# Places, PSUM banks and buffers of the inverse stage in a four-layer convolution chain (fp32)

## The chip, the cores and the metric

One core of one Trainium2 chip runs the whole kernel in one launch. The metric is device time in microseconds (us); the time before is the median of three runs, 2917.45 us (2915.74 to 2919.48). Engines are named as in the profile: PE is the matrix engine (PEld its weight loads), DVE the vector engine, ACT the scalar engine, POOL GpSimd, SP the engine that issues most of the DMA transfers; ACT issues the rest. "ACTq" and "SPq" are the DMA issues of those two.

## The reference, cut to what matters

The input x has 4 images (batches) of 64 channels of 256 x 256, in fp32. Layers 0, 1 and 3 are long convolutions, layer 2 works in a Haar wavelet basis.

```python
# layers 0, 1, 3: a separable filter per channel, hx and hy from a small network
k = einsum('ijk,imk->ijmk', hx, hy)           # one 256x256 kernel per channel
y = irfft2(rfft2(x, pad) * rfft2(k, pad) / n)[:256, :256]
x = y + x * bias
# layer 2
f1 = haar2d(x)
for i in range(2):
    f4 = einsum('bchw,oc->bohw', f1 * v[i], conv_w[i])   # mixes the 64 channels
    acc += sign(f4) * relu(abs(f4) - tau[i])
x = haar2d(acc, inverse=True) + x
```

As every filter is a product of a filter of rows and one of columns, a convolution is two products with Toeplitz matrices, one along each axis. The inverse Haar transform is a product along each axis too.

## The kernel before, in words

A tile holds one channel, 128 partitions x 512 fp32 (256 kB). Four stages follow for each batch:

- `convolutions`: layers 0 and 1 for each channel (products pa0, py0, pa1, py1), then the pair sums along a row. Sums and differences go to the DRAM tensor `keep`; the differences and the further levels are multiplied by a Haar matrix (`down`, PSUM tile pz), copied on ACT into a tile "co" (`away`, L385) and stored in the DRAM tensor `coef`.
- `mixing`: the channels are mixed for each group of coefficients (PSUM tile px) and shrunk. The result stays in SBUF in z.
- `inverse`: for each channel c, `sooner` loads the Toeplitz tile t2 of layer 3, `early` loads r (what `keep` holds), `fetch` copies the channel out of z on ACT (zc, L525, 1.1 us), `rows` makes four products on PE (pw, L532 and L533). For the first 16 channels of a batch `halves` and `cols` follow (pu, L546). `join` on DVE (L554, L557, L558) adds r and undoes the last pair step; its result is the joined tile u.
- `last`: layer 3 on u. It is five steps: "a3" (product pa on PE), "a3 copy" (ACT, L267, into SBUF), "y3" (product py on PE), "y3 sum" (DVE, L284, adds u times the bias), "out" (the store, L599, issued by ACT). In batches 0 to 2 every third channel (`put_off`, c = 2, 5, 8, ...) is not taken through `last` at once: `aside` stores its u in DRAM, and `convolution` takes it up during the mixing of batch 3. In batch 3 nothing is put off.

The convolutions of batch b+1 run beside the mixing of batch b, and their end, with the copies of coefficients, reaches into the inverse stage of batch b.

**Order.** Each step of each channel is an event with a time in ticks: one tick per channel, plus the step's place in the table PLACE. The events are sorted by time and their instructions written in this order; the framework that builds the kernel then sets, from this order and its own estimate, the final order on every engine. Each engine runs its own instructions strictly in that final order, so a waiting instruction holds all that follows it. In the inverse stage of channel c (turn = start + c, one more for c < 16), `rows` stands at 1.071 ticks, `join` at 1.433, a3 at 2.47, y3 and y3 sum at 3.542, out at 4.537.

**PSUM.** [...] The pool psm (L124) has four tiles of one bank, tag "mm", for pa, py, pz, pw and pu. The pool psx (L125) has two tiles of two banks, tag "mix", for the mixing.

**SBUF.** The tag "y" holds the joined tiles u and the y0 of layer 0, in three buffers. The tag "co" holds both the coefficient copies and the y3 of layer 3, in two buffers. The joined sum t has one ("res").

Of the kernel before, what the change touches and what calls it, by code (L numbers as in the profile page):

```python
# [9 lines left out]
F32 = mybir.dt.float32  # L10
# [7 lines left out]
P = 128  # L18
ROW = S + P

GT = 4
BUFS = {"res": 1, "y": 3, "co": 2}

N_ACT = (14, 12, 12, 6)

PLACE = {
    "load": 0.714,
    "a0": 1.643,
    "a0 copy": 1.643,
    "y0": 2.571,  # L30
    "y0 sum": 2.571,
    "a1": 3.5,
    "a1 copy": 3.5,
    "y1": 4.429,
# [64 lines left out]
def conv_seq_kernel(ctx, tc, x, fz, fw, bias, decay, haar, haar_row, factors, vt, taut, wmix, out):  # L99
# [24 lines left out]
    psm = ctx.enter_context(tc.tile_pool(name="psm", bufs=4, space=PSUM))  # L124
    psx = ctx.enter_context(tc.tile_pool(name="psx", bufs=2, space=PSUM))  # L125
# [115 lines left out]
    def toeplitz(layer, c, name):  # L241

        t = tp.tile([P, 2, S], F32, name=name, tag="toep")
        nc.sync.dma_start(t, ap(pads[layer], c * 2 * ROW, [[1, P], [ROW, 2], [1, S]]))
        return t
# [10 lines left out]
    def first(b, st, key, layer, new):  # L256


        def product(c):
            s = st[c]  # L260
            s["p" + new] = bank(f"p{new}_{b}_{c}")
            contract(s["p" + new], s[key], s[layer][:, 0, :])

        def copy(c):
            s = st[c]
            a = s[new] = io.tile([P, 2, S], F32, name=f"{new}_{b}_{c}", tag="mid")
            nc.scalar.copy(a, s["p" + new])  # L267

        return [product, copy]

    def second(b, st, key, layer, res, new, tag, ahead=None):


        def product(c):
            s = st[c]
            if ahead is not None:
                s[ahead] = toeplitz(ahead, c, f"t{ahead}_{b}_{c}")
            s["p" + new] = bank(f"p{new}_{b}_{c}")
            contract(s["p" + new], s[key], s[layer][:, 1, :])

        def residual(c):
            s = st[c]
            y = io.tile([P, 2, S], F32, name=f"{new}_{b}_{c}", tag=tag, bufs=BUFS[tag])
            nc.vector.scalar_tensor_tensor(y, s[res], bsb[:, layer, c : c + 1], s["p" + new], ALU.mult, ALU.add)  # L284
            s[new] = y

        return [product, residual]
# [6 lines left out]
    def level(n, chunk, begin=0, count=None):  # L294

        count = n if count is None else count
        v = z.rearrange("p n s x c -> p n s (x c)")[:, chunk].rearrange("p (j e s) x -> p j e s x", e=2, s=P // 2 // n)
        halve(v[:, begin : begin + count, 0, 0, :], v[:, begin : begin + count, 1, 0, :])

    def butterfly():  # L300

        v = z.rearrange("p n s (h k) c -> p n s h k c", k=2)
        for h in range(2):
            halve(v[:, :, 0, h, 0, :], v[:, :, 0, h, 1, :])
# [6 lines left out]
    def at(time, run, unit):  # L311
        events.append((time, len(events), run, unit))

    def convolutions(b, ticks, in_parts=(), border=None):
# [67 lines left out]
        def away(c):  # L382
            t = io.tile([P, 2, S], F32, name=f"co_{b}_{c}", tag="co", bufs=BUFS["co"])
            ps = parts.pop(("ps", c)).rearrange("p e (k w) -> p e k w", k=2)
            nc.scalar.copy(t.rearrange("p k (e w) -> p e k w", e=2), ps)  # L385
            nc.sync.dma_start(coef[b][:, c].rearrange("k p w -> p k w"), t)
# [122 lines left out]
    def inverse(b, start, put_off):  # L509

        st = {}

        def early(c):
            r = mx.tile([P, 2, 2, P], F32, name=f"r_{b}_{c}", tag="f", bufs=3)
            nc.sync.dma_start(r, keep[b][c])
            st[c]["r"] = r

        def sooner(c):
            st[c] = {}
            if c not in put_off:  # L520
                st[c][2] = toeplitz(2, c, f"t2_{b}_{c}")

        def fetch(c):
            a = mx.tile([P, 2, 2, P], F32, name=f"zc_{b}_{c}", tag="mag")
            nc.scalar.copy(a.rearrange("p h k i -> p (h k) i"), z[:, c // 16, :, :, c % 16].rearrange("p i x -> p x i"))  # L525
            st[c]["z"] = a

        def rows(c):
            a = st[c]["z"]
            ps = psm.tile([P, 2, 2, P], F32, name=f"pw_{b}_{c}", tag="mm")  # L530
            for m in range(2):
                nc.tensor.matmul(ps[:, 0, m, :], a[:, 0, m, :], hsinv, start=True, stop=True)  # L532
                nc.tensor.transpose(ps[:, 1, m, :], a[:, 1, m, :], ident)  # L533
            st[c]["pw"] = ps

        def halves(c):
            w = st[c]["w"] = mx.tile([P, 2, 2, 2, P], F32R, name=f"w_{b}_{c}", tag="f4")
            ps = st[c]["pw"]
            nc.scalar.copy(w[:, 0], ps)
            nc.vector.tensor_tensor(w[:, 1], ps, w[:, 0].bitcast(F32), ALU.subtract)  # L540

        def cols(c):
            ps = psm.tile([P, 2, 2, P], F32, name=f"pu_{b}_{c}", tag="mm")
            flat = "p e m w -> p (e m w)"
            for i in range(2):
                nc.tensor.matmul(  # L546
                    ps.rearrange(flat), hb, st[c]["w"][:, i].rearrange(flat), start=(i == 0), stop=(i == 1)
                )
            st[c]["pw"] = ps

        def join(c):
            ps = st[c]["pw"]
            t = io.tile([P, 2, 2, P], F32, name=f"t_{b}_{c}", tag="res", bufs=BUFS["res"])
            nc.vector.scalar_tensor_tensor(t, st[c]["r"], 0.5, ps, ALU.mult, ALU.add)  # L554
            u = io.tile([P, 2, S], F32, name=f"u_{b}_{c}", tag="y", bufs=BUFS["y"])
            v = u.rearrange("p m (w e) -> p m w e", e=2)
            nc.vector.tensor_add(v[:, :, :, 0], t[:, 0], t[:, 1])  # L557
            nc.vector.tensor_sub(v[:, :, :, 1], t[:, 0], t[:, 1])  # L558
            st[c]["u"] = u

        def aside(c):
            nc.scalar.dma_start(late[b, c], st.pop(c)["u"])

        along = start - groups - 3

        def when(tick, n, chunk, *span):
            at(tick + PLACE["level"], lambda _: level(n, chunk, *span), 0)

        at(along + 11 + PLACE["level"], lambda _: butterfly(), 0)
        for chunk in range(1, 4):  # L570
            turn = start + 16 * (chunk - 1)
            for n in (1, 2, 4, 8):
                when(along + 12 + 3 * chunk if b + 1 < B else turn, n, chunk)
            when(turn + 1, 16, chunk)
            for i in range(2):
                when(turn + 2 + 2 * i, 32, chunk, 16 * i, 16)
            for i in range(4):
                when(turn + 6 + 2 * i, 64, chunk, 16 * i, 16)

        for c in range(C):  # L580
            for name, stage in zip(("sooner", "early", "fetch", "rows"), (sooner, early, fetch, rows)):
                at(start + c + PLACE[name], stage, c)
            turn = start + c
            if c < 16:
                at(start + c + PLACE["halves"], halves, c)
                at(start + c + PLACE["cols"], cols, c)
                turn += 1
            at(turn + PLACE["join"], join, c)
            if c in put_off:
                at(turn + PLACE["aside"], aside, c)  # L590
            else:
                for name, stage in zip(("a3", "a3 copy", "y3", "y3 sum", "out"), last(b, st)):
                    at(turn + PLACE[name], stage, c)

    def last(b, st):
        return [
            *first(b, st, "u", 2, "a3"),
            *second(b, st, "a3", 2, "u", "y3", "co"),
            lambda c: nc.scalar.dma_start(out[b, c].rearrange("(k p) w -> p k w", p=P), st.pop(c)["y3"]),  # L599
        ]  # L600
# [19 lines left out]
    put_off = range(2, C, 3)  # L620
# [22 lines left out]
    for b in range(B):  # L643
        mixing(b, start, N_ACT[b])
        end = start + groups + 3
        if b + 1 < B:
            ready = convolutions(b + 1, spread(ahead, end + 2), in_parts=range(C), border=end)
        else:
            convolution(
                [(i, c) for i in range(B - 1) for c in sorted(put_off)], spread(start - 2, end + 2, (B - 1) * len(put_off))  # L650
            )
        inverse(b, end, put_off if b + 1 < B else ())

        start = max(end + C, ready + 3)
        ahead = start - 3
# [114 lines left out]
```

## Time and profile before

| | |
|---|---|
| median of three runs | 2917.45 us (2915.74 to 2919.48) |
| the profiled execution | 2913.15 us, of it the profile's span 2911.3 us |
| granted clock of PE in it | 0.997 |
| `fetch` zc (ACT, L525), 256 times | 281.5 us, 1101 ns each |
| a copies (ACT, L267), 768 times | 490.7 us, 639 ns each |
| joined tiles (DVE, L554 from pw), 192 times | 131.6 us, 685 ns each |
| y3 sums (DVE, L284 from u), 193 times | 143.9 us, 745 ns each; idle before them 124.6 us |
| pw products (PE, L532 and L533) | 185.9 and 140.4 us |

A group of the profile is one line and one tile of the program on one engine. In the groups all the products of `contract` have the lines L253 and L254, so they are told apart by the tiles: pa from u and py from a in the inverse stage. A bracket at the end of a timeline row gives the idle time before the instruction and what released it; where an instruction waits for several things, the last one by the profile is named. Matrix products are pipelined, so a row's length is longer than its distance to the next row.

### The profile page before, as it was taken

What the parts mean: (1) busy time and instruction counts of PE and PEld (TensorE: products, weight loads), DVE (VectorE), ACT (ScalarE), POOL (GpSimd) and SP (SyncE); (2) the same over time, 40 slices, a digit from 0 to 9 for tenths busy, and PEclk for the clock granted to TensorE, in tenths of its full rate; (3) what the DMA queues carried; (4) which work ended last, traced back from release to release, by engine and by line L of the source; (5) the groups of instructions that cost most, each with busy time, mean ns of one, the idle gap of its engine ahead of it and who ended that gap; (6) DMA issues with size and microseconds to landing.
All of it is one profiled execution on the core that took longest, in us unless ns stands there. A gap on an engine that the chain in (4) does not pass through costs nothing. (4 is left out here: it accounts for less than half of the span.)

```text
span 2911.3 us, 52368 instructions
## 1 busy us (share of the span) xinstructions
PE 2827.3 (97%) x16566; PEld 2551.1 (88%) x16566; DVE 2499.0 (86%) x4263; ACT 2085.2 (72%) x4950; POOL 329.7 (11%) x644
## 2 busy tenths in 40 slices
PE   8999999999999999999999899999999899999999
PEld 6899998888888898998898898998898898887898
DVE  4656558999998679999998679999998779999985
ACT  2333338999995558989985558998986568887554
POOL 0111111121120001221211001121211000000000
PEclk9999999999999999999999999999999999999999
DMA  5878777666676886777677886777777888776676
GB/s 162 256 229 233 231 233 222 205 205 206 197 213 205 268 260 198 214 213 212 208 214 237 253 269 195 214 215 212 208 212 233 262 278 233 235 233 199 208 237 208
DMA packets 599367, 649.77 MB, mean 223 GB/s; under 512 B 48465, under 2 KB 517044, under 8 KB 598964
## 3 DMA queue, kind: packets, MB, share of 16 engines
q1 hardware_dynamic: 519860, 562.09, 65.2%
q10 hardware_dynamic: 79232, 84.34, 8.2%
q8 instruction: 134, 2.20, 0.3%
q14 instruction: 141, 1.16, 0.1%
HBM read 426.77 MB, written 219.48 MB: 222 GB/s over the span
## 5 line engine op out<-in xcount | busy, mean ns | idle before, releaser
L253 PE MATMUL py<-t,a 128*128 128x256 f32 x3072 | 920.9, 382 | 7.5 <-ACT a L267 6.9
L267 ACT COPY a<-pa 128x512 f32<-128x512 f32 x768 | 490.7, 639 | 430.3 <-PE pa L254 390.5
L465 ACT ACTIVATE f<-px,vt 128x64 f32<-128x64 f32 x2816 | 620.2, 408 | 95.9 <-DVE f L460 95.6
L254 PEld LDWEIGHTS py<-t,a 128*128 128x128 f32 x3072 | 584.3, 190 | 79.8
L254 PE MATMUL py<-t,a 128*128 128x128 f32 x3072 | 590.8, 274 | 0.0
L253 PEld LDWEIGHTS py<-t,a 128*128 128x128 f32 x3072 | 496.2, 191 | 47.5 <-ACT a L267 16.8
L441 PE MATMUL px<-wb,f 128*128 128x256 f32 x2048 | 490.4, 381 | 11.1 <-ACT f L465 10.6
L441 PEld LDWEIGHTS px<-wb,f 128*128 128x128 f32 x2048 | 367.7, 190 | 56.4 <-ACT f L465 17.6
L525 ACT COPY zc<-z 128x512 f32<-128x512 f32 x256 | 281.5, 1101 | 170.6 <-PE pw L533 143.6
L343 POOL TENSOR_TENSOR sd<-less 128x128 f32<-128x128 f32 (+4 forms) x320 | 189.3, 592 | 1884.7 <-DVE less L342 1616.8
L469 ACT ACTIVATE mag<-f 128x1024 f32<-128x1024 f32 x256 | 304.1, 1188 | 21.0 <-DVE z L486 20.4
L476 DVE TENSOR_TENSOR mag<-mag,vt 128x1024 f32<-128x1024 f32 x256 | 312.4, 1220 | 4.6 <-ACT mag L469 3.4
L480 DVE SCALAR_TENSOR_TENSOR mag<-mag,f 128x1024 f32<-128x1024 f32 x256 | 312.7, 1222 | 1.1 <-DVE mag L476 0.5
L253 PE MATMUL pa<-t,y 128*128 128x256 f32 x1024 | 308.5, 383 | 4.7 <-DVE y L284 2.9
L253 PE MATMUL pa<-t,x 128*128 128x256 f32 x1024 | 305.7, 380 | 0.0
L366 DVE TENSOR_TENSOR sp<-sd,sp 128x512 fp32r<-128x512 f32 x256 | 179.1, 700 | 135.0 <-ACT sp L361 133.8
L472 ACT ACTIVATE f<-f 128x1024 f32<-128x1024 f32 x256 | 291.4, 1138 | 3.2
L253 PE MATMUL pa<-t,u 128*128 128x256 f32 x772 | 236.0, 388 | 39.2 <-issue 18.9
L284 DVE SCALAR_TENSOR_TENSOR y<-u,bsb,py 128x512 f32<-128x512 f32 x193 | 143.9, 745 | 124.6 <-PE py L254 101.3
L284 DVE SCALAR_TENSOR_TENSOR y<-x,bsb,py 128x512 f32<-128x512 f32 x256 | 189.8, 742 | 42.7 <-PE py L254 41.7
L254 PEld LDWEIGHTS pa<-t,y 128*128 128x128 f32 x1024 | 194.7, 190 | 26.5
L254 PEld LDWEIGHTS pa<-t,x 128*128 128x128 f32 x1024 | 194.6, 190 | 26.3
(72 smaller groups left out, 4450.8 us busy)
## 6 DMA issues: line engine op xcount, KB each, us to landing
t<-pad SPq DMA_DIRECT2D x768, 256.0 KB, 4.0
x<-in_x SPq DMA_DIRECT2D x256, 256.0 KB, 3.8
coef<-co SPq DMA_DIRECT2D x256, 256.0 KB, 3.0
f<-coef SPq DMA_DIRECT2D x256, 256.0 KB, 3.1
r<-keep SPq DMA_DIRECT2D x256, 256.0 KB, 3.7
out_y<-y ACTq DMA_DIRECT2D x256, 256.0 KB, 4.0
keep<-sums SPq DMA_DIRECT2D x256, 128.0 KB, 2.8
keep<-sd SPq DMA_DIRECT2D x256, 128.0 KB, 2.8
```

The lines of the kernel that those rows point to most:

```text
L253: nc.tensor.matmul(ps[:, m, :], src[:, 0, m * P : (m + 1) * P], t[:, ::-1], start=True, stop=False)
L254: nc.tensor.matmul(ps[:, m, P:], src[:, 1, m * P : (m + 1) * P], t[:, : P - 1 : -1], start=False, stop=True)
L267: nc.scalar.copy(a, s["p" + new])
L284: nc.vector.scalar_tensor_tensor(y, s[res], bsb[:, layer, c : c + 1], s["p" + new], ALU.mult, ALU.add)
L343: engine.tensor_tensor(t[:, :, :, half:length], v[..., 0], v[..., 1], ALU.subtract)
L441: nc.tensor.matmul(ps[:, q, h, :], f[:, q, h * P : (h + 1) * P], wb.rearrange("p r n -> p (r n)"), start=True, stop=True,)
L465: nc.scalar.mul(f4[:, j], px[:, j], scale(g, 0)[:, j : j + 1])
L469: nc.scalar.activation(mag, st[g]["f4"], AF.Abs)
L472: nc.scalar.activation(st[g]["f4"], st[g]["f4"], AF.Sign)
L476: nc.vector.tensor_sub(mag, mag, over(g, 1, 16))
L480: nc.vector.scalar_tensor_tensor(mag, mag, 0.0, st[g]["f4"], ALU.max, ALU.mult)
L525: nc.scalar.copy(a.rearrange("p h k i -> p (h k) i"), z[:, c // 16, :, :, c % 16].rearrange("p i x -> p x i"))
```

## The change

Three things, all in the inverse stage: the row products pw take a tile of the mix's PSUM pool and use its first bank; the joined tiles' tag "y" has five buffers in place of three; and the steps of `last` are moved. Where channels are put off, the first of three channels keeps the places of a3 and a3 copy, and has y3, y3 sum and out 0.32 ticks earlier; the second has a3 and a3 copy 0.5 ticks later and y3, y3 sum and out 0.18 ticks later. In batch 3, where nothing is put off, y3, y3 sum and out of every channel come 0.5 ticks earlier.

```diff
-BUFS = {"res": 1, "y": 3, "co": 2}
+BUFS = {"res": 1, "y": 5, "co": 2}
...
         def rows(c):
             a = st[c]["z"]
-            ps = psm.tile([P, 2, 2, P], F32, name=f"pw_{b}_{c}", tag="mm")
+            ps = psx.tile([P, 2, 2, 2, P], F32, name=f"pw_{b}_{c}", tag="mix")[:, 0]
...
             if c in put_off:
                 at(turn + PLACE["aside"], aside, c)
             else:
+                shift = (0.0, -0.32) if c % 3 == 0 else (0.5, 0.18)
+                if not put_off:
+                    shift = (0.0, -0.5)
                 for name, stage in zip(("a3", "a3 copy", "y3", "y3 sum", "out"), last(b, st)):
-                    at(turn + PLACE[name], stage, c)
+                    at(turn + PLACE[name] + shift[name[0] != "a"], stage, c)
```

## The prediction, made before the changed kernel was run

> **What bounds the kernel now.** I read the page's first part, then a table of windows of 20 us, then the timeline inside the windows where TensorE (PE) has gaps, then the idle column of the instruction groups.
>
> ```profile
> PE 2827.3 (97%) x16566; PEld 2551.1 (88%) x16566; DVE 2499.0 (86%) x4263; ACT 2085.2 (72%) x4950; POOL 329.7 (11%) x644
> ...
> 980.00:1000.00 20.00, 16.97 (x108) 15.11 (x109) 14.00 (x28) 11.81 (x15) 0.00 (x0) 1.00 0.74 234
> ...
> 1040.00:1060.00 20.00, 19.82 (x139) 18.55 (x138) 15.38 (x30) 11.73 (x13) 0.00 (x0) 1.00 0.90 284
> ...
> 2840.00:2860.00 20.00, 20.00 (x137) 18.75 (x136) 12.68 (x24) 10.35 (x13) 0.00 (x0) 1.00 0.78 244
> ```
>
> PE sets the time, and only its gaps can be won: 84 us in all. A window row gives the stretch, then busy PE, PEld, DVE, ACT and POOL, the granted clock, the DMA share and GB/s. The change touches only the inverse stages: batch 0 near 880-1080, batch 1 near 1540-1740, batch 2 near 2200-2400, batch 3 near 2680-2907. From the rows, PE idles 13.6, 10.7 and 10.4 us in the first three and 4.5 us in the last (all of it before 2800). I split the first three: phase A (channels below 16, with the column products) holds 13.1 us, phase B (the coefficient copies of the next batch still run) 21.4 us, phase C (after them) 0.2 us. So the whole prize is about 35 us, and phases C and the last 100 us of the kernel can only lose.
>
> Phase B, from the timeline (start, length, engine, line):
>
> ```profile
> 984.30 0.59 ACT L385 COPY co<-pz 128x512 f32<-128x512 f32 x1 [1.19 <-PE pz L373]
> ...
> 984.91 0.37 SPq L386 DMA_DIRECT2D coef<-co  x1
> ...
> 988.72 0.75 DVE L284 SCALAR_TENSOR_TENSOR y<-u,bsb,py 128x512 f32<-128x512 f32 x1 [1.02 <-DMA coef<-co]
> ...
> 989.49 0.38 ACTq L599 DMA_DIRECT2D out_y<-y  x1
> ...
> 990.24 0.67 PE L253 MATMUL pa<-t,u 128*128 128x256 f32 x2 [1.00 <-PE pw L533]
> ```
>
> The result tile y3 and the coefficient tile share the tag "co" with two buffers. The second y3 of three channels waits for the coefficient store (988.72), DVE stands behind it, the next join is late, and PE waits 1.00 us. The cycle of three channels is 9.30 us (984.30 to the next such copy at 993.60), while PE's own work is 3 rows of 0.66 + 4 products of 1.31 + 0.55 for pz = 7.8 us (start-to-start distances in the timeline).
>
> **The change, part by part.** No instruction is added or removed; only order, banks and buffers move.
>
> *Five joined tiles.* What the third buffer cost is bounded by the row of the join:
>
> ```profile
> L557 DVE TENSOR_TENSOR u<-t 128x256 f32<-128x256 f32 x256 | 108.2, 423 | 6.7 <-DMA late<-u 1.2
> ```
>
> A join that waits for an old u to be stored shows 1.2 us in the whole run: worth 0 to -1.2 us, I take 0. Its effect is indirect: joins may run further ahead.
>
> *Row results in the mix banks.* Before, four banks serve 8 tiles per three channels (3 pw, 2 pa, 2 py, 1 pz); afterwards they serve 5, and pw has two tiles of its own, which the mix leaves unused here. rows(c) then waits for join(c-2), placed 1.64 ticks earlier, so nothing new is on the path; at the borders the first pw waits until the mix's last tile is read and the next mix's first tile waits for the join of channel 62, both done a tick before (0 to +1 us per border, taken as 0). Gain: part of phase A, where PE waits for u behind a DVE that is busy 18.8 to 19.9 of 20 us (860-900). More banks don't shorten DVE. Bounds -9 and +3 us (the latter from the shorter covers below); I take -3.
>
> *Even spacing, batches 0 to 2.* The places become a3 at 2.47 and 3.97, y3 at 3.222 and 4.722 ticks. That spreads the two y3, but it also shortens what PE has between a3 and y3 of one channel. In the built order of PE, before: another product and a row product (1.97 us). After: in phase C a row product and a third (0.88 us) for one channel, one and a half (0.99 us) for the other. What is needed shows where the trace has the two products back to back:
>
> ```profile
> 2669.33 0.39 PE L254 MATMUL pa<-t,v 128*128 128x128 f32 x2
> ...
> 2669.75 0.58 ACT L267 COPY a<-pa 128x512 f32<-128x512 f32 x1 [0.70 <-PE pa L254]
> ...
> 2670.39 0.70 PE L253 MATMUL py<-t,a 128*128 128x256 f32 x2 [0.68 <-ACT a L267]
> ```
>
> pa's stream ends at 2669.55 (it began at 2668.24, plus 1.31); the copy starts 0.20 later (0.25 in the last stage: 2898.79 against 2898.54), lasts 0.58, and py starts 0.06 after it, with its first pair 0.1 longer. So a cover of x us leaves PE idle about 1.0 - x. Phase C: 0.12 us in each of some 9 cycles, three batches: **+3 us** (0 to +6).
>
> Phase B after the change. PE's loop: 7.8 + 0.35 (cover 0.66) + 0.12 (cover 0.88) = 8.25 us, because DVE's waiting y3 now holds the join of a product that stands later on PE. The loop over the one shared buffer stays, as the change adds none: copy to y3 4.42 us (984.30 to 988.72), y3 to its store 0.77, the store's landing 2.7 (median of 975-1010), then the next copy: 7.9 us. But a faster stage loads the DMA: 9 transfers of 262 kB in 8.25 us are 286 GB/s. The row for that is 1040-1060 (284 GB/s, share 0.90), and out_y lands there after 4.9 us: the loop is then 10.1 us, no gain. So between -1.05 and 0 per cycle, about 18 cycles in three batches (4, 7 and 7 gaps of this kind): -19 to 0. I take -0.45 per cycle, **-8 us**, since loop and load must meet between 8.25 and 9.3.
>
> [...] The rows agree that a buffer is short, but it is "co", not "y" or PSUM[...]. [...] The landing times above already stretch from 2.7 to 4.9 us at 284 GB/s, so I follow the rows.
>
> *Even spacing, batch 3.* Nothing is put off there, y3 moves 0.5 tick forward: 0.57 tick behind its own a3. In the built order before, PE runs row(c+1), a3(c), y3(c-1): a3 is covered by 3.28 us. After: a3(c), one row product, y3(c), and for the last six channels (58-63) a3 and y3 with nothing between, as the rows now run six channels ahead. The trace of before in this stage:
>
> ```profile
> 2842.47 0.38 PE L254 MATMUL pa<-t,u 128*128 128x128 f32 x2
> ...
> 2842.69 0.60 PE L253 MATMUL py<-t,a 128*128 128x256 f32 x2
> ...
> 2842.95 0.58 ACT L267 COPY a<-pa 128x512 f32<-128x512 f32 x1 [0.22 <-PE pa L254]
> ```
>
> PE goes straight on with the py of another channel at 2842.69; if it were its own, a would be there at 2843.6. On ACT, the store of an earlier y3 and the next fetch (1.10 us) stand around the copy, but the store's y3 is done a product earlier and the fetch fits behind, so the copy starts at once. SP's queue: a t2 load waits for the py six channels earlier, and r loads stand behind it; in the new order both are still issued four channels (13 us) before use and land in 3.8 us, cost 0. Channels 37-57: 21 x 0.34 = 7.1 us; 36: 0.2; 58-63: 6 x 1.0 = 6.0; together 13 us in a stretch where PE is 20.00 of 20. Channels 0-31 lose 9 us by the same count, but there DVE is full (20.00 of 20 at 2700-2740) and PE has 4.5 us idle and slower matmuls (123 to 130 in 20 us instead of 136), so most is hidden: +3. **+16 us**, bounds +8 (ACT and PE overlap better than in the row) and +24 (nothing hidden).
>
> Sum: -3 + 3 - 8 + 16 = +8 us. The profiled execution took 2913.15 us (span 2911.3, 1.85 us around it) and would become 2921. Its time lies 4.3 us below the median 2917.45; on the median the forecast is 2926.
>
> **The rivals.**
> *Phase B wins all, and batch 3 hides half*: -17 (landings stay at 2.7 us), -6 in A, +2, +8: -13, so **2904**. For it: the loop of 7.9 us as measured, DMA share only 0.74 in the worst window. Against: the landing of 4.9 us. It decides once three channels take under 8.6 us in phase B.
> *The parts cancel*: phase B -8, batch 3 only +8, A and C zero: **2917**. For it: ACT is half idle in batch 3. Against: the latency row, which is ACT-free too.
> *ACT's order costs more*: in phase B the store of the second y3 now stands ahead of the next a3 copy, so a wait for "co" holds ACT and PE instead of a fetch. One landing of 4.9 us delays that copy by up to 1 us past its cover: B +3, batch 3 +22, C +4: +29, **2947**. Against: that copy is not due before 6.15 us into the cycle, the store is issued by 6.
>
> **How the numbers follow.** Main case 0.49 (own range 2919 to 2934), all of B won 0.18, cancel 0.21, ACT's order 0.12. Within 0.2% means 2911.6 to 2923.3, about what a measurement of this kernel can tell from no change. Slower: 0.12 + most of the main case + a tail of cancel, 0.57; same 0.24; faster 0.19. The range 2905 to 2944 cuts half of the two outer cases.
>
> **What would show it.** Batch 3: idle before py, released by ACT's a, of about 0.3 us per channel, near 1 us in the last six, the windows after 2800 at 18 of 20. Phase B: copies of co 8.5 to 9 us apart instead of 9.3, y3 still released by coef or out_y, out_y landing later. Phase C full within 2%. I am wrong if py in batch 3 shows no wait for a, or if phase B falls to 8.3 us.

## The result, and the profile after

The changed kernel takes 2917.12 us (median of 14 runs, 2914.62 to 2921.9) against 2916.57 us before (14 runs): ratio 1.000, 95% interval 0.9992 to 1.0009. No difference can be measured. The profiled execution took 2915.48 us, its span is 2913.7 us (before 2911.3), and the granted clock rose from 0.997 to 1.000.

The unchanged sum hides two large changes that cancel. The marks of the trace cut the span into stages: the first copy of a channel out of z (L525) begins an inverse stage, the first instruction of the next mixing (L452) or the end of the span ends it. The mixing stages are the same within 0.8 us.

| inverse stage, us | batch 0 | batch 1 | batch 2 | batch 3 |
|---|---|---|---|---|
| before | 211.4 | 209.1 | 203.4 | 235.6 |
| after | 203.2 | 205.2 | 202.4 | 251.3 |
| difference | -8.2 | -3.9 | -1.0 | +15.7 |

One stage of one execution is good to about 3 us: batch 2, 203.4 us before, took 206.8 us in the run below that moves steps of batch 3 alone.

First the busy totals of the page and the table of windows, both after (columns as before: busy PE, PEld, DVE, ACT, POOL, then clock, DMA share, GB/s):

```profile
PE 2837.4 (97%) x16566; PEld 2548.3 (87%) x16566; DVE 2504.6 (86%) x4263; ACT 2081.6 (71%) x4950; POOL 329.1 (11%) x644
...
980.00:1000.00 20.00, 18.66 (x122) 16.80 (x121) 14.10 (x28) 12.51 (x16) 0.00 (x0) 1.00 0.86 271
...
1040.00:1060.00 20.00, 20.00 (x138) 18.83 (x137) 15.13 (x30) 12.12 (x15) 0.00 (x0) 1.00 0.92 290
...
2840.00:2860.00 20.00, 19.67 (x123) 17.31 (x122) 11.77 (x22) 8.92 (x11) 0.00 (x0) 1.00 0.78 221
```

The first window gained (122 matrix products in place of 108), the second kept its pace, the last one lost: 123 products in place of 137, though PE still counts as busy for 19.67 us. Read the count, not the busy time: rows of products are longer than the distance between them (the row at 2841.99 below takes 0.39 us, the next begins 0.22 us after it), so a short wait disappears in the overlap. The weight loads (PEld) show a part of it, 17.31 us in place of 18.75. The groups of the page (busy time, mean ns | idle before, releaser) name what is late, first before, then after:

```profile
L253 PE MATMUL py<-t,a 128*128 128x256 f32 x3072 | 920.9, 382 | 7.5 <-ACT a L267 6.9
...
L253 PE MATMUL pa<-t,u 128*128 128x256 f32 x772 | 236.0, 388 | 39.2 <-issue 18.9
```

```profile
L253 PE MATMUL py<-t,a 128*128 128x256 f32 x3072 | 929.8, 384 | 32.1 <-ACT a L267 28.8
...
L253 PE MATMUL pa<-t,u 128*128 128x256 f32 x772 | 231.4, 381 | 1.5 <-PE pw L533 0.7
```

The wait has moved from the first product of a channel (pa) to the second (py), which needs the copy a. The timeline of batch 3 after (start, length, engine, line) shows one channel and the next:

```profile
2841.99 0.39 PE L254 MATMUL pa<-t,u 128*128 128x128 f32 x2
2842.21 0.39 PE L532 MATMUL pw<-hrow,zc 128*128 128x128 f32 x2
2842.47 0.59 ACT L267 COPY a<-pa 128x512 f32<-128x512 f32 x1 [1.87 <-PE pa L254]
...
2843.10 0.30 PEld L253 LDWEIGHTS py<-t,a 128*128 128x128 f32 x2 [0.30 <-ACT a L267]
2843.10 0.70 PE L253 MATMUL py<-t,a 128*128 128x256 f32 x2
...
2846.08 0.59 ACT L267 COPY a<-pa 128x512 f32<-128x512 f32 x1 [1.87 <-PE pa L254]
```

From copy to copy it is 3.61 us. Before, it was 3.28 us, from the copy at 2842.95 that the prediction shows to the next:

```profile
2846.23 0.58 ACT L267 COPY a<-pa 128x512 f32<-128x512 f32 x1 [0.22 <-PE pa L254]
```

After, only the row product (0.66 us) stands between a3 and y3 of one channel, py starts 0.04 us after its copy has ended, and 0.33 us per channel are lost. The product py carries no bracket, so no idle time is put down to it; its weight load waited 0.30 us for ACT's a.

The starts of the y3 sums (DVE) split the last inverse stage by channels:

| batch 3, us | before | places put back (first run below) | after |
|---|---|---|---|
| first copy to y3 of channel 31 | 129.1 | 121.9 | 131.3 |
| channels 31 to 36 | 16.4 | 16.4 | 18.3 |
| channels 36 to 57 | 69.0 | 69.0 | 76.1 |
| channels 57 to 63 | 17.1 | 17.1 | 21.7 |
| from there to the end | 4.1 | 4.1 | 3.9 |

### The profile page after: what moved, and what is told of

Read it like the earlier page. It is cut to its first block, busy times and chain, and to the rows that moved or that the text cites. A ratio compares the mean times of both kernels' runs of the same rounds, so it can differ in the third digit from the quotient of the medians.

```text
span 2913.7 us, 52472 instructions
## 1 busy us (share of the span) xinstructions
PE 2837.4 (97%) x16566; PEld 2548.3 (87%) x16566; DVE 2504.6 (86%) x4263; ACT 2081.6 (71%) x4950; POOL 329.1 (11%) x644
## 5 line engine op out<-in xcount | busy, mean ns | idle before, releaser
L525 ACT COPY zc<-z 128x512 f32<-128x512 f32 x256 | 279.7, 1101 | 49.5 <-PE pw L533 38.0
```

## The experiments

Differences in us are worked out from the ratio, as (ratio - 1) x 2917. Edits are shown against the kernel before, except where the text says against the changed kernel.

**Batch 3's places put back** (against the changed kernel).

```diff
                 if not put_off:
-                    shift = (0.0, -0.5)
+                    shift = (0.0, 0.0)
```

> The changed kernel with the places of batch 3 as they were before (a3 at 2.47, y3 at 3.542); banks, buffers and the spacing of batches 0 to 2 stay. Theory (a3's copy lost its cover in batch 3): the inverse stage of batch 3 falls back from 251.3 to about 235.6 us, py waits for a only a few us, the whole is 14 to 16 us faster than the changed kernel: 2901 to 2903. Rival (the loss in batch 3 comes from the row products' two tiles or from joins that run ahead): the stage stays near 250 us and the time near 2917.

2893.06 us, ratio 0.992 (0.9906 to 0.9935): -23 us against the kernel before, more than the theory's 14 to 16. Its last stage took 228.4 us in place of 251.3, the first three 203.3, 206.6 and 199.9. So batch 3's places cost 22.9 us, and the other parts of the change won as much, 7 us of it in the last stage, where the theory had expected nothing from them.

**Batch 3's places alone.**

```diff
+                shift = (0.0, 0.0)
+                if not put_off:
+                    shift = (0.0, -0.5)
...
-                    at(turn + PLACE[name], stage, c)
+                    at(turn + PLACE[name] + shift[name[0] != "a"], stage, c)
```

> The kernel before with only y3, y3 sum and out of batch 3 half a tick earlier. Theory: in the built order y3 then follows its own a3 on PE with nothing between, for nearly all 64 channels; at 1.0 us each, less some 10 us hidden behind DVE before 2800, the stage grows by 40 to 55 us: about 2960 to 2970. Rival (the places cost nothing by themselves): within 5 us of 2917.

2971.25 us, ratio 1.0183 (1.0168 to 1.0198): +53 us; the last stage took 290.3 us, 54.7 more than before. In the timeline of this run nothing stands between the two products of a channel:

```profile
2862.30 0.38 PE L254 MATMUL pa<-t,u 128*128 128x128 f32 x2
2862.78 0.59 ACT L267 COPY a<-pa 128x512 f32<-128x512 f32 x1 [0.20 <-PE pa L254]
2863.42 0.70 PE L253 MATMUL py<-t,a 128*128 128x256 f32 x2 [0.73 <-ACT a L267]
...
2867.06 0.59 ACT L267 COPY a<-pa 128x512 f32<-128x512 f32 x1 [0.20 <-PE pa L254]
```

A channel takes 4.28 us, 1.00 more than 3.28. Together with the 3.61 us above (cover 0.66, loss 0.33) this is the prediction's rule, idle = 1.0 - cover, at two points. Counted over all 64 channels in the built order it gives 23.0 us for the changed kernel (measured 22.9) and 61 for this one (54.7; the rest is missing among the channels up to 31, which lost 21 us of the 29 counted). Why the same places leave a cover in the one and none in the other: with pw in banks of its own, the builder sets a row product between the two; that was read from the built order, not tried.

**Banks and five tiles, no step moved.**

```diff
-BUFS = {"res": 1, "y": 3, "co": 2}
+BUFS = {"res": 1, "y": 5, "co": 2}
...
-            ps = psm.tile([P, 2, 2, P], F32, name=f"pw_{b}_{c}", tag="mm")
+            ps = psx.tile([P, 2, 2, 2, P], F32, name=f"pw_{b}_{c}", tag="mix")[:, 0]
```

> The kernel before with the row products in the mix's banks and five joined tiles, all places as before. Theory (the gain of batches 0 to 2 comes from the spacing in phase B, and banks help phase A only): 2 to 5 us faster, 2912 to 2915, with copies of co still about 9.3 us apart in phase B. Rival (banks and buffers make the gain): 12 to 15 us faster, near 2903, copies of co 8.3 to 8.6 us apart.

2902.14 us, ratio 0.9945 (0.9932 to 0.9958): -16 us. The theory missed and the rival's value came, but not the rival's mark: in phase B the coefficient copies come 9.84 us apart (mean of three gaps per batch; 9.52 before), so this gain lies outside phase B.

**Even spacing of batches 0 to 2 alone.**

```diff
+                shift = (0.0, -0.32) if c % 3 == 0 else (0.5, 0.18)
+                if not put_off:
+                    shift = (0.0, 0.0)
...
-                    at(turn + PLACE[name], stage, c)
+                    at(turn + PLACE[name] + shift[name[0] != "a"], stage, c)
```

> The kernel before with only the spacing of batches 0 to 2. Theory: phase B wins as in the changed kernel, but with the row products back in the common banks PE has just one row product (0.66 us) between a3 and y3 of every channel, 0.35 us lost each, some 6 us per batch in phase C: -8 + 15, about +5 to +10, 2922 to 2927. Rival (spacing alone makes the gain): 8 to 13 us faster, 2904 to 2909.

2922.02 us, ratio 1.0012 (1.0003 to 1.0020): +3.5 us. Alone the spacing is a small loss. With banks and tiles it wins: 0.992 against 0.9945, some 7 us, though the two intervals just meet. The theory had both halves, with a sum just below its 5 to 10: in phase B the coefficient copies come 8.82 us apart in place of 9.52, and phase C loses. In this run the built order leaves 0.66 us between a3 and y3 of every channel, and where the coefficient copies have ended, PE makes 383, 411 and 320 products in stretches (1005-1066, 1665-1730, 2320-2370 us) that held 410, 440 and 340 before; the changed kernel, with more cover, makes 413, 435 and 340.

**Banks alone, and five tiles alone.** 
```diff
-            ps = psm.tile([P, 2, 2, P], F32, name=f"pw_{b}_{c}", tag="mm")
+            ps = psx.tile([P, 2, 2, 2, P], F32, name=f"pw_{b}_{c}", tag="mix")[:, 0]
```

```diff
-BUFS = {"res": 1, "y": 3, "co": 2}
+BUFS = {"res": 1, "y": 5, "co": 2}
```

> The kernel before with the row products in the mix banks alone: three joined tiles, no place moved. Banks and buffers together gave -14.5 us against the kernel before (2902.1 against about 2916.6), -6.8 of it in the last inverse stage by the stage times and about -5 in the first three. Theory 'the banks make that gain': 2902 to 2905, last inverse stage near 229 us instead of 235.6. Rival 'the five joined tiles make it': 2914 to 2917, last inverse stage near 235. If both are needed together (joins run ahead only when pw has banks of its own and u has tiles): 2908 to 2914 here and 2915 to 2917 with five tiles alone.

> The kernel before with five joined tiles alone. PE's order is the same as before; only the order of some DVE instructions in the convolutions' end and the waits for old joined tiles differ. Theory 'the banks make the gain of banks and buffers': 2915 to 2917, no change, as the prediction's row of 1.2 us says. Rival 'the tiles make it': 2902 to 2905.

Banks: 2902.46 us, ratio 0.9953 (0.9940 to 0.9965), -14 us. Tiles: 2912.33 us, ratio 0.9984 (0.9978 to 0.9991), -5 us, a small gain that the row of 1.2 us did not show. So the banks make most of the gain. Whether the tiles add to it the times can't tell: both together gave -16 us, and the interval, -20 to -12, holds -14 as well as -19. In the last stage the tiles do add: it took 232.8 us with the banks alone (229 was expected), 232.5 with the tiles alone and 228.8 with both; the four other runs with the banks, four or five tiles and batch 3's old places lie between 228 and 230 us, the five with neither between 234.8 and 235.6. What the tiles change there was not followed; they leave the order on PE as it was and change that on DVE at 114 of 4263 places. Part of the banks' gain can be seen at the start of batch 3. The timeline and the window there, before:

```profile
2675.72 2.08 ACT L525 COPY zc<-z 128x512 f32<-128x512 f32 x2 [1.82 <-DVE z L486]
2676.86 0.80 PE L532 MATMUL pw<-hrow,zc 128*128 128x128 f32 x2 [3.58 <-ACT zc L525]
...
2678.30 1.06 PE L253 MATMUL py<-t,a 128*128 128x256 f32 x2
```

```profile
2672.00:2683.00 11.00, 7.42 (x31) 6.63 (x30) 10.81 (x14) 5.23 (x8) 0.00 (x0) 0.69 0.37 110
```

and with the banks alone:

```profile
2669.54 0.60 PE L253 MATMUL py<-t,a 128*128 128x256 f32 x2
...
2671.70 0.49 PE L532 MATMUL pw<-hrow,zc 128*128 128x128 f32 x2 [1.33 <-ACT zc L525]
...
2673.71 0.59 PE L253 MATMUL pa<-t,v 128*128 128x256 f32 x2
```

```profile
2666.00:2678.00 12.00, 9.64 (x60) 8.18 (x59) 11.91 (x19) 8.96 (x12) 0.00 (x0) 1.00 0.59 161
```

Before, the first row product stands ahead of a py whose input is ready (its copy ended at 2673.89), waits 3.58 us for the first copy out of z, and the products behind it are slow: a pair of 128x256 takes 1.06 us in place of 0.60, the granted clock of the window is 0.69. With the banks that py goes first, PE idles 1.33 us, and the clock of the window is 1.00. The first y3 of the stage comes 13.4 us after the first copy, in place of 16.7: 3.3 us. How much of this is the clock can be read from a run further down, the third shared buffer. Its PE runs in the order of before and waits as long at this place, but the clock stays at 1.00:

```profile
2653.15 0.49 PE L532 MATMUL pw<-hrow,zc 128*128 128x128 f32 x2 [3.59 <-ACT zc L525]
```

```profile
2653.15:2658.15 5.00, 4.92 (x32) 4.45 (x33) 5.00 (x6) 3.14 (x4) 0.00 (x0) 1.00 0.18 51
```

There the first y3 comes after 15.6 us, and the stage takes 234.8 us in place of 235.6. So the slow products are an estimated 1.1 us of the 3.3 (16.7 less 15.6), and less than 1 us of the stage; the rest of the 3.3 us goes with the order.

The first three stages together are 4.4 us shorter with the banks alone (619.5 against 623.9), with 31 or 32 products in place of 26 or 27, and of 21, in the two slices of 5 us of batches 1 and 2 in which PE has its first gaps. With 2.8 us in the last stage that is 7.2 us; the traces do not place the other half of the 14 us, as the profiled execution of before lies 3.7 us below its median and that of this run 2.7 us above. Where that half sits stays open.

**A buffer of its own for y3.**

```diff
-BUFS = {"res": 1, "y": 3, "co": 2}
+BUFS = {"res": 1, "y": 3, "co": 2, "yo": 2}
...
-            *second(b, st, "a3", 2, "u", "y3", "co"),
+            *second(b, st, "a3", 2, "u", "y3", "yo"),
```

> The kernel before with a tag of its own (two buffers) for the y3 of layer 3, so that coefficient copies and y3 no longer wait for each other's stores; PE's order is unchanged. Theory 'the shared tag sets phase B' (the prediction's loop of 7.9 to 10.1 us): the coefficient copies of the first inverse stage come 8.0 to 8.6 us apart instead of 9.3, no y3 in that stretch is released by coef, and the first three stages together lose 10 to 18 us: 2899 to 2907. Rival 'the transfers themselves set phase B': copies stay 9.0 to 9.3 apart and y3 waits for its own older store: 2912 to 2917. Rival 'PE's order sets it': no wait of y3 is left, the join is still late, 2912 to 2917.

2888.23 us, ratio 0.990 (0.9887 to 0.9914): -29 us, more than the theory's 10 to 18. The coefficient copies come 8.13 us apart in phase B, as the theory had it. The first three stages took 202.2, 200.1 and 195.6 us (9.2, 9.0 and 7.8 less), the last 235.5, where no coefficient copies are left. The order of PE's instructions is that of before.

**A third shared buffer; and one copy buffer with two for y3.**

```diff
-BUFS = {"res": 1, "y": 3, "co": 2}
+BUFS = {"res": 1, "y": 3, "co": 3}
```

```diff
-BUFS = {"res": 1, "y": 3, "co": 2}
+BUFS = {"res": 1, "y": 3, "co": 1, "yo": 2}
```

> The kernel before with three buffers for the shared tag of coefficient copies and y3. The order on every engine is that of the run with a tag of its own for y3 (2888.2 us); only the waits for old buffers differ. Theory 'the loop over the two shared buffers costs, and one more breaks it': the copies of phase B come 8.1 us apart as there, 2887 to 2892. Rival 'it is the mixing of two kinds in one ring that costs, however many buffers': still 9.0 or more apart, 2905 to 2917.

> The kernel before with two buffers of their own for y3 and only one for the coefficient copies: three in all. Same order on every engine as with two and two (2888.2 us). Theory 'y3's wait for the coefficient store is what counts': 2887 to 2891, since in phase B the copies come one in 8.1 us and each store lands within 3 to 6 us. Rival 'the copies need two buffers': where two copies follow within a channel (before phase B) ACT waits a landing of 3 to 5 us for the first: 2893 to 2905.

Third shared buffer: 2888.45 us, ratio 0.9893 (0.9877 to 0.9910), -31 us. One number in one line wins what the separate tag wins. One copy buffer: 2895.76 us, 0.9916 (0.9902 to 0.9931), -25 us; the inverse stages are as short as with two, but the first mixing starts at 454.0 us of the trace in place of 450.8 and lasts 2 to 3 us longer, so the rival came, near the small end of its range. Phase B with the third shared buffer, first the windows, then the timeline:

```profile
980.00:1000.00 20.00, 19.76 (x132) 18.04 (x131) 15.62 (x31) 13.60 (x17) 0.00 (x0) 1.00 0.91 286
1000.00:1020.00 20.00, 20.00 (x141) 18.88 (x140) 15.05 (x31) 12.49 (x15) 0.00 (x0) 1.00 0.95 303
```

```profile
988.25 0.59 ACT L385 COPY co<-pz 128x512 f32<-128x512 f32 x1 [1.19 <-PE pz L373]
...
990.79 0.74 DVE L284 SCALAR_TENSOR_TENSOR y<-u,bsb,py 128x512 f32<-128x512 f32 x1
...
995.92 0.75 DVE L284 SCALAR_TENSOR_TENSOR y<-u,bsb,py 128x512 f32<-128x512 f32 x1 [1.21 <-PE py L254]
996.38 0.59 ACT L385 COPY co<-pz 128x512 f32<-128x512 f32 x1 [1.19 <-PE pz L373]
```

The copies come 8.13 us apart in all three batches, the second y3 of the three channels (990.79) waits for nothing, and 132 products stand where there were 108. The transfers did not become faster: in 960-1005 us the stores of y3 land after 4.7 us (median) and those of coefficients after 5.1, against 4.4 and 4.4 before. They are just not waited for. (With a buffer of its own for y3 as with the third shared one, the builder also sets some y3 sums ahead of a join, which changes DVE's order at 30 of 4263 places; the orders on PE and ACT are those of before. That order and the missing wait come together and were not parted.)

**All but batch 3's places, with a tag of its own for y3; then the same with no step moved.** Both have the row products in the mix banks, four joined tiles, one copy buffer and two for y3. Against the changed kernel:

```diff
-BUFS = {"res": 1, "y": 5, "co": 2}
+BUFS = {"res": 1, "y": 4, "co": 1, "yo": 2}
...
-                    shift = (0.0, -0.5)
+                    shift = (0.0, 0.0)
...
-            *second(b, st, "a3", 2, "u", "y3", "co"),
+            *second(b, st, "a3", 2, "u", "y3", "yo"),
```

and the second without the lines of `shift`.

> The changed kernel with the last inverse stage's places put back, four joined tiles, one buffer for the coefficient copies and two of their own for y3. With the places put back alone it was 2893.1. Theory 'the shared tag still costs after the change': phase B goes from copies 8.3 to 9.0 apart to about 8.0 to 8.25, some 0.5 us in each of 18 cycles: -5 to -9, 2884 to 2888. Rival 'after the even spacing nothing waits for the shared tag any more': 2892 to 2895. Rival 'one buffer for the coefficient copies is too few' (each copy waits for the landing of the one before, 3 to 5 us, and two copies follow each other within a channel): slower than 2897.

> The best version so far (2876.4 us) without its places: the kernel before with the row products in the mix banks, four joined tiles, one buffer for coefficient copies and two of their own for y3, all steps where they stood before. Theory 'once the shared buffer is gone, the places have nothing left to win': banks alone gave -14.4 and the tag alone -28.6; if they add, 2873 to 2877. Rival 'the even spacing still pays when the waits are gone' (it paid 9 us with the banks: 2893.1 against 2902.1): 2882 to 2888. Rival 'banks and tag win the same idle time': 2884 to 2889, the same number, told apart by phase B: copies 8.1 apart for this one against above 8.4 for the other.

2876.39 us, ratio 0.9861 (0.9848 to 0.9875), and without the places 2877.28 us, ratio 0.9853 (0.9838 to 0.9868). The first is 17 us faster than the run with batch 3's places put back (2893.06 us), so the shared buffer still cost that one some 17 us, more than the 5 to 9 expected, and once it is gone the even spacing is worth nothing. Spacing and buffer seem to win the same idle time; banks and buffer add, within the intervals (-14 for the banks, -25 to -29 for y3's own tag, -43 together with four joined tiles).

**The version that beats both: banks, four joined tiles, third shared buffer, nothing moved.**

```diff
-BUFS = {"res": 1, "y": 3, "co": 2}
+BUFS = {"res": 1, "y": 4, "co": 3}
...
-            ps = psm.tile([P, 2, 2, P], F32, name=f"pw_{b}_{c}", tag="mm")
+            ps = psx.tile([P, 2, 2, 2, P], F32, name=f"pw_{b}_{c}", tag="mix")[:, 0]
```

> The kernel before with the row products in the mix banks, four joined tiles and three buffers for the shared tag of coefficient copies and y3; no step is moved. Same order on every engine as the run with banks and own tags and no places (2877.3 us), whose single copy buffer cost ACT waits before the first mixing (there the first mixing starts at 453.8 us of the trace instead of 450.8, and the first one lasts as long as before). Theory 'the third shared buffer is enough, and the copies are free again': 3 us better, 2872 to 2876, first mixing at 450 to 451. Rival 'with the joins earlier three shared buffers are again too few for copies and y3 together': y3 released by coef in phase B, 2878 to 2888.

2871.54 us (2865.8 to 2873.07), ratio 0.9845 (0.9831 to 0.9858): -45 us. The windows of phase B and the group of pa:

```profile
960.00:980.00 20.00, 20.00 (x133) 18.55 (x132) 15.35 (x31) 14.17 (x18) 0.00 (x0) 1.00 0.94 299
980.00:1000.00 20.00, 20.00 (x136) 18.55 (x135) 15.73 (x31) 12.69 (x15) 0.00 (x0) 1.00 0.93 288
```

```profile
L253 PE MATMUL pa<-t,u 128*128 128x256 f32 x772 | 233.8, 385 | 2.4 <-PE pw L533 1.8 <-issue 0.4
```

PE is full there, idle time before pa is 2.4 us in place of 39.2, and the clock is 1.000.

## Why the prediction was right or wrong, point by point

The time, 2917.1 us, lies in the range; the likeliest case, 2926, did not come. The value is that of "the parts cancel", but not for that case's reason: batch 3 lost 15.7 us, not 8. That the time lies in the range is in part luck. The runs put -16 us on banks and tiles (predicted -3), some -7 on the even spacing (predicted -5) and +23 on batch 3's places (predicted +16): two errors, of 13 and of 7 us, with opposite signs.

- **Batch 3, +16: right in mechanism, and its total right by two errors.** The places cost 22.9 us. Behind channel 31 the table shows 7.1 us for channels 36 to 57, as predicted to the tenth; 1.9 before them and 4.6 behind (predicted 0.2 and 6.0), 13.6 in all against 13. The term "most is hidden: +3" failed: channels up to 31 lost 9.4 us (131.3 against 121.9), all that the cover count gave. That DVE was busy there hid nothing in this kernel; it hid 8 of 29 us where nothing at all stood between the products. Of the signs, idle time before py released by a came, the windows at 18 of 20 did not: the wait hides in the rows. The other error is in the next point: the prediction gave the banks nothing in this stage, and banks and tiles won 7.2 us there (235.6 to 228.4).
- **Banks, -3 with bounds -9 and +3: failed.** Alone they win 14 us (10 to 17). "At the borders 0 to +1 us per border, taken as 0" is one term: at the last border the first y3 comes 3.3 us sooner, because the builder's order there changes and, for an estimated 1.1 us of it, because the slow products are gone (the clock of the window is 1.00 in place of 0.69). The row that told it, 3.58 us in front of pw, was in the trace but in no sum: the wait ends at 2676.86, and the prediction's last stage starts at 2680. Its "4.5 us in the last" are other gaps, 4.0 us of them between 2740 and 2760. Where half of the 14 us sits stays open.
- **Five tiles, 0 to -1.2 us: too small alone** (-5 us). On top of the banks the times can't tell, and the last stage shows some 4 us (232.8 to 228.8). The waits that are put down to an old u, 1.2 us, bound only one of the ways in which the tiles act; the others were not followed.
- **Phase B, -8: right.** Over three gaps per batch the copies came 9.52 us apart before and 8.94 after: 0.58 x 18 = 10 us. It is the spacing that does it (8.82 alone; 9.84 with banks and tiles and no spacing). That the loop over the two shared buffers stays, and that the even spacing can win only part of it, is what the third buffer showed. The second reason fell: that the DMA load keeps the stage above 8.25 us. It ran at 8.04 to 8.13 us with 286 to 303 GB/s (and at 7.87 us with the even spacing and a tag of its own for y3). So 286 GB/s left room here. The row was right that landings are long there (4.7 to 5.1 us), but the 2.7 us that the prediction set against them are three stores; over 960-1005 us the median is 4.4 before, too. With two buffers the landings are waited for, with three not. The choice of the tag in phase B was right: "co", not "y". PSUM was not out of it altogether, as the banks won 14 us elsewhere.
- **Phase C, +3: not seen.** 435 products against 440 in batch 1, the same or more in the others; too small for these counts. The mechanism itself shows in the spacing alone, where cover is shorter.
- **The prize, 35 us: too small.** The best version wins 45. Its first three stages are 36.8 us shorter (587.1 against 623.9), close to what the rows gave; 7.5 us more come from the last stage, which the prize left out.

So the sum of +8 failed at the terms for banks and tiles (-3 in place of -14 to -16) and for the hidden part of batch 3 (+3 in place of +9.4). The rival "all of B won" needed another change: one more buffer, not other places.

## What to carry to other kernels

Where an engine waits for the landing of a store, count the buffers of that ring before steps are moved: here one more won 31 us, and the places that went around it 7 at best. Before a consumer is moved nearer to its producer, count the work that stands between them on the bounding engine in the built order; each channel here lost about 1.0 us minus that work, and a busy DVE hid none of it in one run and 8 of 29 us in the other. In a window, read the number of products and the clock beside the busy time.

## What the runs showed of the hardware that was not expected

The granted clock fell for a short stretch. In the profile of the kernel before, a pair of 128x256 took 1.06 us in place of 0.60 from 2676.86 to about 2682.4 us, behind 3.58 us of idle time, and the granted clock of this stretch was 0.50. The length of the gap alone did not decide it. At the same place 3.59 us left the clock at 1.00 with the third shared buffer, and the pair at 0.60 with the even spacing alone. In the profile of before, pairs of 1.06 us came behind 2.69 us of idle time at 907.5 us too (clock 0.66 in the 5 us from there), while behind 2.10 us at 2278.2 the pair took 0.67 (clock 1.00 in the 5 us from there). What set the clock no run here shows. In 5.54 us at a clock of 0.50 PE lost an estimated 2.8 us beyond the gap itself, of which less than 1 us was left at the end of the stage (235.6 us, and 234.8 with the third shared buffer).
